# VectorE's tanh rows with the bias in a PSUM bank, and layer 0 through two-bank tiles

## The chip, the cores and the metric

The kernel runs on one core of a Trainium2 chip. Five engines work side by side, each through its own queue in order: TensorE (PE) multiplies matrices into PSUM, VectorE (DVE), ScalarE (ACT) and GpSimd (POOL) work elementwise, and SyncE (SP) starts transfers. Engines wait for one another by semaphores. PSUM is eight banks of 128 partitions by 512 float32 values. The metric is the device time of the whole program in microseconds; lower is better. Everything is float32.

## What is computed

Eight batches of N = 1024 tokens with C = 128 channels pass two layers. Cut to what matters:

```python
# layer 0, per batch, 8 heads; 1024 keys = 64 (m) x 16 (g)
scores = einsum('bhlfc,bhmgc->bhlfmg', q, k) / sqrt(c)
a = softmax(scores, axis=4)        # over m
a = softmax(a, axis=5)             # over g
z = einsum('bhlfmg,bhmgc->bhlfc', a, v)
z1 = layer_norm(z @ wo.T + bo + x)
x = layer_norm(relu(z1 @ w1.T + b1) @ w2.T + b2 + z1)

# layer 1, attention: every pair of tokens i, j
Wi = B @ W.T                       # B: normalised tokens
scores = einsum('d,bijd->bij', v, tanh(Wi[:, None] + Wi[:, :, None]))
t = t + softmax(scores) @ B

# layer 1, recurrence over the 1024 tokens
y = sigmoid(wx_t + y @ V.T)
```

The costly parts are layer 0's double softmax (8 x 8 x 1024 x 1024 scores) and layer 1's tanh of every pair's sum in 128 channels. The pair matrix is symmetric, so only its upper half is computed.

## The kernel before

**Two layers at once.** The kernel doesn't run its loops in order. Functions layer0(b) and layer1(b) only register operations in a Plan (add): which engines may do it and at what cost in us, which keys it reads and writes, its priority, and which tile of a choice (Bank) it takes or gives back. When all are registered, Plan.emit plays a list scheduler at build time: at each step it takes the engine that can start first and, among its ready operations, the one of lowest priority number, and issues it there. So each engine's order is fixed when the program is built, from the costs written in the code, and layer 0 of batch b + 1 is woven among layer 1 of batch b. An operation that gives several engines goes to the one that can start it first. Operations marked port on VectorE and all of GpSimd are planned never to overlap (port_free).

**Layer 0.** For each head the query projection u (L833, evicted with its bias at L837 or L839) and the values (L847, copied at L793 or L795) are made. Then for each tile of 128 queries: scores into a PSUM tile sc of two banks (L869, two matmuls of 512 columns); exponential in place in PSUM (L872, ACT); sums over m and their reciprocal (L876, L877, VectorE), division from PSUM into the SBUF tile e (L880, VectorE). For each pair of such tiles: exponential (L890), sums over g and reciprocal (L893, L894), division on GpSimd (L904), transposes in groups of four through one PSUM bank (L783) and copies out (L795), the product with the values (L918) and its addition to zs (L925). There are two score tiles sc0 and sc1, used in turn, two single banks m0 and m1 for every other product (the choice called two), and two pairs of e tiles. Batch 0's first half runs before any layer 1, and may also use the two banks of sa and the ACT engine for its copies. through_bank is the helper that does a matmul into a bank and its eviction; most products go through it. Batches 0 and 7 do the upper half of their queries first.

**Layer 1's tanh rows.** For each tile it of 128 tokens (w = 1024 - 128 it columns remain), group(...) handles k tokens of each of four interleaved columns c, where k = max(1, 1024 // w): 1, 1, 1, 1, 2, 2, 4, 8 for the eight tiles. Its 4k rows of sums Wi[j] + Wi[i] are written into one of five row slots th, 4096 columns wide. The first of four operations, one for each c, settles whether ACT makes the whole group (tanh_row, L1029: a tanh with the row's own column as bias, one instruction a row) or whether GpSimd and VectorE make the sums, c by c: add_rows (L1039, one instruction for k rows) on GpSimd, and on VectorE where k is 4 or more, which is then marked port; add_row (L1033, one accumulating instruction a row) on VectorE where k is below 4. Sums made there go through one wide tanh (wide_tanh, L1087, ACT). Then times_v (L1107, PE) multiplies by the vector v into the PSUM tile sa of two banks, four column groups side by side, and gives the slot back. After a tile pair's rows comes the exponential from sa to E (L1203), transposes and the product with B (L1236). The result, and layer 1's projections, use the same single banks.

**After the batches** the recurrence runs over all tokens in 32 chunks side by side (L1419, L1421).

PSUM is full: sa 2 banks, sc0 and sc1 2 each, m0 and m1 1 each.

Of the kernel before, what the change touches and what calls it, by code (L numbers as in the profile page):

```python
# [565 lines left out]
def fast_path(ctx: ExitStack, tc: tile.TileContext, a: dict, fits):  # L566
# [67 lines left out]
    m1 = tile_of(psum, "m1", [P, 512])  # L634
    two = (("m0", m0), ("m1", m1))
    four = two + (("sa0", sa[:, 0:512]), ("sa1", sa[:, 512:1024]))
# [82 lines left out]
    for h in range(H):  # L719
        nc.tensor.matmul(m1[:, 0:1], wo[:, h, :], bvn[:, h : h + 1], start=h == 0, stop=h == H - 1)  # L720
    nc.vector.scalar_tensor_tensor(zb, m1[:, 0:1], float(M), bo, ALU.mult, ALU.add)
# [51 lines left out]
    def through_bank(pe, weight, r, evict, where, more, w, pri, choice=two):  # L773

        bank = Bank(*choice)
        n = len(plan.ops)
        add(("PE", weight), lambda _: pe(bank()), r=r, w=[("bank", n)], pri=pri, take=bank, wait=more + w)
        add(where, lambda e: evict(e, bank()), r=[("bank", n)] + more, w=w, pri=pri, give=bank)
# [8 lines left out]
    def copy(dst):  # L787
        def fn(e, bank):
            src = bank
            if len(dst.shape) == 3:  # L790
                src = bank[:, : dst.shape[1] * P].rearrange("p (t c) -> p t c", c=P)
            if e == "ACT":
                nc.scalar.activation(dst, src, AF.Copy)  # L793
            else:
                nc.vector.tensor_copy(dst, src)  # L795
# [6 lines left out]
    def layer0(b):  # L802
# [16 lines left out]
        for n_part, part in enumerate(parts):  # L819
            qts = range(NT) if part is None else range(4 * part, 4 * part + 4)  # L820

            banks = four if alone and n_part == 0 else two
            for h in range(H):
# [5 lines left out]
                for s in range(2) if part is None else (part,):  # L829
                    cols = slice(s * 512, (s + 1) * 512)  # L830

                    def project(bank, h=h, cols=cols):
                        nc.tensor.matmul(bank, A[:, h, :], xT[:, cols], start=True, stop=True)  # L833

                    def biased(e, bank, h=h, u=u, cols=cols):
                        if e == "ACT":
                            nc.scalar.activation(u[:, cols], bank, AF.Identity, bias=ub[:, h : h + 1])  # L837
                        else:
                            nc.vector.tensor_scalar(u[:, cols], bank, ub[:, h : h + 1], None, ALU.add)  # L839

                    through_bank(project, 0.9, [kx], biased, evict(0.75), [], [("u", h % 2, s)], L0, banks)
                for s in () if alone and n_part else range(2):

                    def values(bank, h=h, s=s):
                        for i in range(4):
                            t = 4 * s + i
                            nc.tensor.matmul(  # L847
                                bank[:, i * P : (i + 1) * P], xT[:, t * P : (t + 1) * P], Wvo[:, h, :], start=True, stop=True
                            )

                    through_bank(
                        values, 0.95, [kx], copy(vp[:, 4 * s : 4 * s + 4, :]), evict(0.68), [], [kvp + (s,)], L0, banks
                    )
                for qt in qts:
                    L0 = pace(n_part, h + (qt - qts[0]) / len(qts))
                    i = (n_part * H + h) * len(qts) + qt - qts[0]
                    sc, kc = scs[i % 2], ("sc", i % 2)
# [4 lines left out]
                    r1, r2 = st[:, q, 0:G], st[:, :, G : G + M]  # L862
                    sc3 = sc.rearrange("p (m g) -> p m g", g=G)
                    e3 = e.rearrange("p (m g) -> p m g", g=G)

                    def scores(_, sc=sc, u=u, qt=qt):
                        for s in range(2):
                            cols = slice(s * 512, (s + 1) * 512)
                            nc.tensor.matmul(sc[:, cols], u[:, qt * P : (qt + 1) * P], xT[:, cols], start=True, stop=True)  # L869

                    add(("PE", 1.74), scores, r=[kx, ("u", h % 2, qt // 4)], w=[kc], pri=L0)
                    add(("ACT", 0.98), lambda _, sc=sc: nc.scalar.activation(sc, sc, AF.Exp, scale=SCALE),  # L872
                        r=[kc], w=[kc], pri=L0)

                    def first_sums(_, sc=sc, r1=r1):
                        nc.vector.tensor_reduce(r1, sc.rearrange("p (m g) -> p g m", g=G), AX.X, ALU.add)  # L876
                        nc.vector.reciprocal(r1, r1)  # L877

                    def divide(_, e3=e3, sc3=sc3, r1=r1):
                        nc.vector.tensor_tensor(e3, sc3, r1.unsqueeze(1).to_broadcast([P, M, G]), ALU.mult)  # L880

                    add(("DVE", 1.49), first_sums, r=[kc], w=[k1], pri=L0)
                    add(("DVE", 1.22), divide, r=[kc, k1], w=[ke], pri=L0)
# [15 lines left out]
                    for q in range(2):  # L899
# [7 lines left out]
                        for s in range(2):  # L907
                            through_bank(
                                transposes([e[:, t * P : (t + 1) * P] for t in range(4 * s, 4 * s + 4)]), 0.52, [ke],
                                copy(aT[:, 4 * s : 4 * s + 4, q * P : (q + 1) * P]), evict(0.68), [],  # L910
                                [("aT", na, q, s)], L0, banks,
                            )
# [14 lines left out]
                    for s in range(2):  # L927
                        add(
                            ("PE", 1.74), lambda _, attend=attend, s=s: attend(s),
                            r=[kvp + (p,) for p in range(2)] + [("aT", na, q, p) for q in range(2) for p in range(2)],  # L930
# [5 lines left out]
            for qh in range(2) if part is None else (part,):  # L936
# [24 lines left out]
                kh = [("aT", na, q, s) for q in range(2) for s in range(2)]  # L961
                for f in range(NFF):

                    def hidden(bank, f=f, z1T=z1T):
                        nc.tensor.matmul(bank, w1_sb[:, f * P : (f + 1) * P], z1T, start=True, stop=True)

                    def relu(e, bank, f=f, hT=hT):
                        if e == "ACT":
                            nc.scalar.activation(hT[:, f, :], bank, AF.Relu, bias=b1_sb[:, f : f + 1])
                        else:  # L970
                            nc.vector.tensor_scalar(hT[:, f, :], bank, b1_sb[:, f : f + 1], 0.0, ALU.add, ALU.max)

                    through_bank(hidden, 0.9, [k1], relu, evict(0.75), kh[:1] if f else [], kh if f == 0 else [kh[f]], L0, banks)
# [20 lines left out]
                add(("PE", 5.4), outer, r=kh + [k1], w=[kb], pri=L0, take=bank, wait=[kg])  # L994
# [8 lines left out]
    unused = stats[5][:, 3, 8:9]  # L1003
    slots = [(f"th{s}", ths[s]) for s in range(5)]

    def group(it, at0, r0, k, wiT, all_wi, L1, ROWS, fillers, chain, left, both, first_half):
# [9 lines left out]
        slot = Bank(*slots[: 3 if first_half else 5])  # L1016

        begin = [0 if r0 == 0 else 4 * r0 + c for c in range(4)]
        at = [k * sum(w - q for q in begin[:c]) for c in range(5)]

        def rows(c):
            return slot()[:, at[c] : at[c + 1]].rearrange("p (r n) -> p r n", r=k)

        def w_i(c, r=None):
            j = i0 + 4 * r0 + c
            return wiT[:, j : j + 4 * k - 3 : 4] if r is None else wiT[:, j + 4 * r : j + 4 * r + 1]

        def tanh_row(c, r):
            nc.scalar.activation(rows(c)[:, r, :], wiT[:, i0 + begin[c] :], AF.Tanh, bias=w_i(c, r))  # L1029

        def add_row(c, r):

            nc.vector.tensor_scalar(  # L1033
                rows(c)[:, r, :], wiT[:, i0 + begin[c] :], w_i(c, r), 0.0, ALU.add, ALU.add, accum_out=unused
            )

        def add_rows(eng, c):
# [472 lines left out]
```

## Time and profile before

| | us |
|---|---|
| median of 3 runs | 5395.53 (5393.81 to 5401.85) |
| profiled execution | 5395.36 |
| its span | 5393.6 |
| ACT wide tanh, L1087, x953 | 2629.0 |
| ACT tanh row by row, L1029, x2084 | 1502.5 |
| POOL row adds, L1039, x2268 | 3318.7 |
| DVE row adds one by one, L1033, x1754 | 1542.3 |
| DVE first sums, L876, and division, L880, x512 each | 619.7 and 624.2 |
| DVE copies of 512 columns to aT, L795, x927 | 600.3 |
| PE row products, L1107 | 2037.4 |

The chip's profiler records every instruction with its engine, start and duration. A group's row gives line, engine, operation, what it writes and reads (out<-in), how often, then busy time and mean duration, then the idle time of the engine just before such instructions and what ended most of it. An arrow <- names what was waited for. A float32 matmul appears as two PE instructions in most groups. Busy times are of one execution, and idle time of an engine that isn't the limit costs nothing.

### The profile page before, as it was taken

What the parts mean: (1) busy time and instruction counts of PE and PEld (TensorE: products, weight loads), DVE (VectorE), ACT (ScalarE), POOL (GpSimd) and SP (SyncE); (2) the same over time, 40 slices, a digit from 0 to 9 for tenths busy, and PEclk for the clock granted to TensorE, in tenths of its full rate; (3) what the DMA queues carried; (4) which work ended last, traced back from release to release, by engine and by line L of the source; (5) the groups of instructions that cost most, each with busy time, mean ns of one, the idle gap of its engine ahead of it and who ended that gap; (6) DMA issues with size and microseconds to landing.
All of it is one profiled execution on the core that took longest, in us unless ns stands there. A gap on an engine that the chain in (4) does not pass through costs nothing.

```text
span 5393.6 us, 99434 instructions
## 1 busy us (share of the span) xinstructions
PE 5044.0 (94%) x39173; PEld 2771.6 (51%) x39173; DVE 4933.6 (91%) x8326; ACT 5099.2 (95%) x4190; POOL 4496.0 (83%) x3078
## 2 busy tenths in 40 slices
PE   8999999999999999999999999999999999995566
PEld 6655554555555455555555555545555455542125
DVE  7998989899999999899998999999998999999886
ACT  5489999999999999999999999999999999999994
POOL 2364779798989899899998989898898998996992
PEclk9999999999999999999999999999999999998999
DMA  2000000000000000000000000000000000000001
GB/s 62 1 5 1 1 1 5 1 9 1 1 5 6 4 1 1 5 9 1 1 5 5 5 1 1 5 5 5 1 1 3 7 1 1 1 30 8 1 1 68
DMA packets 27341, 37.73 MB, mean 7 GB/s; under 512 B 2512, under 2 KB 19280, under 8 KB 26864
## 3 DMA queue, kind: packets, MB, share of 16 engines
q1 hardware_dynamic: 24832, 27.99, 1.6%
q8 instruction: 310, 5.08, 0.4%
q10 hardware_dynamic: 1872, 3.16, 0.2%
q14 instruction: 167, 1.37, 0.1%
q0 software_dynamic: 160, 0.13, 0.0%
HBM read 19.22 MB, written 12.06 MB: 6 GB/s over the span
## 4 chain that ended last, share of the span: by engine, by line
PE 56%; ACT 19%; DVE 18%; issue 6%; POOL 1%; DMA 0%; DVEq 0%; ACTq 0%; SPq 0%; POOLq 0%
PE sa L1107 20%; PE m L918 11%; PE sc L869 10%; ACT th L1087 10%; PE m L783 6%; ACT th L1029 5%; DVE th L1033 5%; DVE stat_e L876 2%; DVE stat_e L893 2%; DVE wx L880 2%; ACT sc L872 2%; ACT wx L890 2%; PE m L1236 2%; DVE aT L795 2%; PE m L847 1%
## 5 line engine op out<-in xcount | busy, mean ns | idle before, releaser
L1039 POOL TENSOR_TENSOR th<-wiT 128x1024 f32<-128x1024 f32 (+54 forms) x2268 | 3318.7, 1500 | 318.2 <-PE sa L1107 298.8
L1087 ACT ACTIVATE th<-th 128x4096 f32<-128x4096 f32 (+55 forms) x953 | 2629.0, 2788 | 22.6 <-DVE th L1039 9.5
L1107 PE MATMUL sa<-th,vpat 128*32 128x512 f32 (+33 forms) x24576 | 2037.4, 462 | 235.6 <-ACT th L1087 223.3
L1033 DVE TENSOR_SCALAR_CACHE_REDUCE th<-wiT 128x512 f32<-128x512 f32 (+57 forms) x1754 | 1542.3, 879 | 156.7 <-PE sa L1107 40.3
L1029 ACT ACTIVATE th<-wiT 128x384 f32<-128x384 f32 (+60 forms) x2084 | 1502.5, 792 | 29.2 <-PE sa L1107 28.9
L1107 PEld LDWEIGHTS sa<-th,vpat 128*32 128x32 f32 x24576 | 662.8, 110 | 1372.1 <-issue 844.3
L904 POOL TENSOR_TENSOR wx<-wx,stat_e 128x1024 f32<-128x1024 f32 x512 | 983.9, 1944 | 389.4 <-DVE stat_e L894 320.8
L869 PE MATMUL sc<-xT,wx 128*128 128x512 f32 x2048 | 981.2, 604 | 11.3 <-DVE wx L880 10.7
L918 PE MATMUL m<-aT,wx 128*128 128x256 f32 x3584 | 823.7, 383 | 4.7 <-DVE aT L795 4.5
L918 PEld LDWEIGHTS m<-aT,wx 128*128 128x128 f32 x3584 | 668.1, 190 | 187.5 <-issue 48.0
L880 DVE TENSOR_TENSOR wx<-sc,stat_e 128x1024 f32<-128x1024 f32 x512 | 624.2, 1219 | 25.0
L876 DVE TENSOR_REDUCE stat_e<-sc 128x16 f32<-128x1024 f32 x512 | 619.7, 1210 | 25.8 <-ACT sc L872 25.3
L795 DVE COPY aT<-m 128x512 f32<-128x512 f32 x927 | 600.3, 674 | 36.7 <-PE m L783 34.3
L783 PEld LDWEIGHTS m<-ident,wx 128*128 128x128 f32 x3940 | 443.5, 141 | 326.0 <-issue 156.9
L893 DVE TENSOR_REDUCE stat_e<-wx 128x128 f32<-128x2048 f32 x256 | 583.2, 2278 | 19.1 <-ACT wx L890 18.4
L783 PE MATMUL m<-ident,wx 128*128 128x128 f32 x3940 | 562.6, 278 | 29.7 <-DVE aT L795 14.3
L872 ACT ACTIVATE sc<-sc 128x1024 f32<-128x1024 f32 x512 | 512.7, 1007 | 62.3 <-PE sc L869 56.0
L869 PEld LDWEIGHTS sc<-xT,wx 128*128 128x128 f32 x2048 | 354.7, 190 | 374.4 <-issue 329.3
L890 ACT ACTIVATE wx<-wx 128x2048 f32<-128x2048 f32 x256 | 487.7, 1905 | 30.1 <-DVE wx L880 29.9
L894 DVE RECIPROCAL stat_e<-stat_e 128x128 f32<-128x128 f32 x256 | 243.9, 953 | 8.8
L847 PEld LDWEIGHTS m<-Wvo,xT 128*128 128x128 f32 x1080 | 134.4, 192 | 53.0 <-issue 26.9
L847 PE MATMUL m<-Wvo,xT 128*128 128x128 f32 x1080 | 145.5, 281 | 4.4 <-DVE aT L795 2.4
(183 smaller groups left out, 2887.0 us busy)
## 6 DMA issues: line engine op xcount, KB each, us to landing
xT<-in_xt_dram SPq DMA_DIRECT2D x8, 512.0 KB, 3.6
th<-in_x_dram SPq DMA_DIRECT2D x8, 512.0 KB, 6.8
parked<-X SPq DMA_DIRECT2D x16, 256.0 KB, 2.3
xr<-parked SPq DMA_DIRECT2D x8, 512.0 KB, 8.1
parked_wx<-bT SPq DMA_DIRECT2D x14, 256.0 KB, 2.0
wx<-parked_wx SPq DMA_DIRECT2D x7, 512.0 KB, 4.3
out_dram<-ot ACTq DMA_DIRECT2D x8, 256.0 KB, 2.1
out_dram<-ot SPq DMA_DIRECT2D x8, 256.0 KB, 2.8
```

The lines of the kernel that those rows point to most:

```text
L783: nc.tensor.transpose(bank[:, i * P : (i + 1) * P], s, ident)
L795: nc.vector.tensor_copy(dst, src)
L869: nc.tensor.matmul(sc[:, cols], u[:, qt * P : (qt + 1) * P], xT[:, cols], start=True, stop=True)
L876: nc.vector.tensor_reduce(r1, sc.rearrange("p (m g) -> p g m", g=G), AX.X, ALU.add)
L880: nc.vector.tensor_tensor(e3, sc3, r1.unsqueeze(1).to_broadcast([P, M, G]), ALU.mult)
L904: nc.gpsimd.tensor_tensor(e3, e3, r2[:, q, :].unsqueeze(2).to_broadcast([P, M, G]), ALU.mult)
L918: nc.tensor.matmul(bank()[:, :256], vp[:, t, :], aT[:, t, :], start=t == 0, stop=t == NT - 1)
L1029: nc.scalar.activation(rows(c)[:, r, :], wiT[:, i0 + begin[c] :], AF.Tanh, bias=w_i(c, r))
L1033: nc.vector.tensor_scalar(rows(c)[:, r, :], wiT[:, i0 + begin[c] :], w_i(c, r), 0.0, ALU.add, ALU.add, accum_out=unused)
L1039: eng.tensor_tensor(rows(c), wiT[:, i0 + begin[c] :].unsqueeze(1).to_broadcast(shape), w_i(c).unsqueeze(2).to_broadcast(shape), ALU.add,)
L1087: nc.scalar.activation(slot()[:, a:z], slot()[:, a:z], AF.Tanh)
L1107: nc.tensor.matmul(sa[32 * c : 32 * c + 32, s:s1], vpat[:, 31 - r0 - r : 63 - r0 - r], rows(c)[:, r, s - at0 - begin[c] : s1 - at0 - begin ...
```

## The change

**The bank near.** m1 goes. In its place stands near, one PSUM bank. Its first 64 columns hold layer 0's reciprocals of the first sums; seven areas of 64 columns hold copies of a row tile's own columns of Wi, written by VectorE for each half tile of 64 tokens, in turn. In the profile's operations only VectorE touches it, but for one small product before the plan starts.

**Rows.** VectorE's add is now a tensor_tensor of a broadcast column from near (PSUM) and the other tokens (SBUF), with several rows in one instruction: per = 1, 1, 1, 2, 2, 4, 8, 16 rows for tiles 0 to 7, whoever makes them. A group is cut into 4k / per pieces instead of four, its rows lie token after token, all as long as the longest, and one tanh covers the whole slot. VectorE's row operations are no longer marked port. The matmuls take the same rows at their new places.

**Layer 0.** The first exponential goes from the score tile to e in SBUF, and the score tile is free after it. First sums read e, the reciprocal goes to near, and the division works on e in place. Scores come from the choice called two, which is now sc0 and sc1; so do the eight transposes of a query tile together, the values of a head together, the projection where both halves are made at once, and pairs of hidden products. Each is evicted by one instruction (relu by two) over 1024 columns. Everything narrow takes any of m0, sc0 and sc1. Batch 0's first half may also use sa as a third wide tile.

```diff
+    near = tile_of(psum, "near", [P, 512])
+    two = tuple((f"sc{i}", t) for i, t in enumerate(scs))
+    three = two + (("sa", sa),)
+    any_of = (("m0", m0),) + two
...
-                    sc, kc = scs[i % 2], ("sc", i % 2)
-                    r1, r2 = st[:, q, 0:G], st[:, :, G : G + M]
+                    s1, r2 = st[:, q, 0:G], st[:, :, G : G + M]
+                    r1 = near[:, (2 * pair + q) * G : (2 * pair + q + 1) * G]
...
-                    add(("PE", 1.74), scores, r=[kx, ("u", h % 2, qt // 4)], w=[kc], pri=L0)
-                    add(("ACT", 0.98), lambda _, sc=sc: nc.scalar.activation(sc, sc, AF.Exp, scale=SCALE),
-                        r=[kc], w=[kc], pri=L0)
-                        nc.vector.tensor_reduce(r1, sc.rearrange("p (m g) -> p g m", g=G), AX.X, ALU.add)
-                        nc.vector.reciprocal(r1, r1)
-                        nc.vector.tensor_tensor(e3, sc3, r1.unsqueeze(1).to_broadcast([P, M, G]), ALU.mult)
+                    through_bank(
+                        scores, 1.74, [kx, ("u", h % 2, qt // 4)],
+                        lambda _, bank, e=e: nc.scalar.activation(e, bank, AF.Exp, scale=SCALE), ("ACT", 0.98), [], [ke], L0, wide,
+                    )
+                        nc.vector.tensor_reduce(s1, e.rearrange("p (m g) -> p g m", g=G), AX.X, ALU.add)
+                        nc.vector.reciprocal(r1, s1)
+                        nc.vector.tensor_tensor(e3, r1.unsqueeze(1).to_broadcast([P, M, G]), e3, ALU.mult)
...
-                        for s in range(2):
-                            through_bank(
-                                transposes([e[:, t * P : (t + 1) * P] for t in range(4 * s, 4 * s + 4)]), 0.52, [ke],
-                                copy(aT[:, 4 * s : 4 * s + 4, q * P : (q + 1) * P]), evict(0.68), [],
-                                [("aT", na, q, s)], L0, banks,
-                            )
+                        through_bank(
+                            transposes([e[:, t * P : (t + 1) * P] for t in range(NT)]), 1.04, [ke],
+                            copy(aT[:, :, q * P : (q + 1) * P]), evict(1.24), [], [("aT", na, q)], L0, wide,
+                        )
...
-            nc.vector.tensor_scalar(
-                rows(c)[:, r, :], wiT[:, i0 + begin[c] :], w_i(c, r), 0.0, ALU.add, ALU.add, accum_out=unused
-            )
+        if 4 * r0 % 64 == 0:
+            n = count.setdefault("near", 0)
+            count["near"] = n + 1
+            count["near", it] = n % 7
+            cols, own = near[:, 64 * (n % 7 + 1) : 64 * (n % 7 + 2)], wiT[:, i0 + 4 * r0 : i0 + 4 * r0 + 64]
+            add(("DVE", 0.15), lambda _, cols=cols, own=own: nc.vector.tensor_copy(cols, own), r=all_wi,
+                w=[("near", n % 7)], pri=ROWS - 0.03)
+        kn = ("near", count["near", it])
+        biases = near[:, 64 * (kn[1] + 1) : 64 * (kn[1] + 2)]
+        W = w - 4 * r0
+        per = (1, 1, 1, 2, 2, 4, 8, 16)[it]
+        pieces = 4 * k // per
...
+        def add_rows(e, p):
+            shape = [P, per, W]
+            others = wiT[:, i0 + 4 * r0 :].unsqueeze(1).to_broadcast(shape)
+            if e == "DVE":
+                own = biases[:, 4 * r0 % 64 + p * per : 4 * r0 % 64 + (p + 1) * per].unsqueeze(2).to_broadcast(shape)
+                nc.vector.tensor_tensor(rows(p), own, others, ALU.add)
+            else:
+                own = w_i(p * per, per).unsqueeze(2).to_broadcast(shape)
+                nc.gpsimd.tensor_tensor(rows(p), others, own, ALU.add)
...
         work = {
-            "ACT": lambda c: (k * (0.18 + 0.833e-3 * (w - begin[c])), lambda: [tanh_row(c, r) for r in rows_of]),
-            "POOL": lambda c: (0.27 + 1.62e-3 * k * (w - begin[c]), lambda: add_rows(nc.gpsimd, c)),
-            "DVE": lambda c: (k * (0.21 + 1.05e-3 * (w - begin[c])), lambda: [add_row(c, r) for r in rows_of])
-            if k < 4
-            else (0.15 + 1.04e-3 * k * (w - begin[c]), lambda: add_rows(nc.vector, c)),
+            "ACT": (per * (0.18 + 0.833e-3 * W), lambda p: [tanh_row(j) for j in rows_of(p)]),
+            "POOL": (0.27 + 1.62e-3 * per * W, lambda p: add_rows("POOL", p)),
+            "DVE": (0.15 + 1.04e-3 * per * W, lambda p: add_rows("DVE", p)),
         }
```

## The prediction

> **What bounds the kernel now.** I read the page's busy shares first, then the same per stretch (windows), then the groups of the stretch from 310 to 4650 us, then those of the end, and last the durations of single lines.
>
> ```profile
> PE 5044.0 (94%) x39173; PEld 2771.6 (51%) x39173; DVE 4933.6 (91%) x8326; ACT 5099.2 (95%) x4190; POOL 4496.0 (83%) x3078
> ```
>
> Four engines lie between 83 and 95%, so no share alone tells the bound. The windows do (columns: stretch, length, then busy us and instructions of PE, PEld, DVE, ACT, POOL, the granted clock, DMA):
>
> ```profile
> 0.00:100.00 100.00, 91.27 (x449) 69.88 (x450) 67.94 (x87) 62.04 (x180) 26.94 (x25) 1.00 0.30 83
> ...
> 200.00:310.00 110.00, 101.04 (x449) 67.20 (x447) 98.50 (x138) 57.85 (x66) 47.12 (x32) 1.00 0.00 1
> ...
> 2000.00:2500.00 500.00, 490.52 (x3804) 266.80 (x3802) 464.18 (x790) 495.47 (x390) 460.27 (x317) 1.00 0.01 4
> ...
> 4700.00:4900.00 200.00, 169.92 (x1464) 84.26 (x1466) 186.39 (x456) 192.19 (x153) 173.37 (x126) 0.95 0.08 25
> ...
> 5000.00:5100.00 100.00, 59.82 (x536) 16.39 (x536) 84.19 (x152) 100.00 (x34) 90.46 (x57) 0.98 0.00 1
> ```
>
> The reader sees four regimes. Start, 0 to 310: layer 0 of batch 0 alone; PE 91%, DVE 90% once loaded. Middle, 310 to 4700: PE 98% and ACT 99% together, DVE 93%, POOL 92%. End, 4700 to 5300: only layer 1 of batch 7 is left at last; ACT near 100%, PE 60%. From 5300 the recurrence, untouched. Summed over its windows, PE is busy 4278.6 of the middle's 4390 us: 111 us idle. Which waits those are, and who else waits, is in the groups of 310 to 4650:
>
> ```profile
> L1039 POOL TENSOR_TENSOR th<-wiT 128x832 f32<-128x832 f32 (+54 forms) x1915 | 2812.2, 1505 | 248.1 <-PE sa L1107 239.5 <-ACT th L1029 5.2 <-ACT sc L872 1.5
> L1107 PE MATMUL sa<-th,vpat 128*32 128x512 f32 (+36 forms) x20688 | 1692.0, 458 | 56.3 <-ACT th L1087 53.6 <-ACT E L1203 1.6 <-ACT th L1029 0.8
> L869 PE MATMUL sc<-xT,wx 128*128 128x512 f32 x1792 | 859.5, 604 | 9.3 <-DVE wx L880 9.1
> L783 PE MATMUL m<-ident,wx 128*128 128x128 f32 x3588 | 512.7, 278 | 23.4 <-DVE aT L795 12.4 <-DVE wx L839 4.4 <-POOL E L1209 2.6
> ```
>
> POOL waits 240 us for PE to give a row slot (th) back, so the rows are made faster than PE eats them: PE is the bound of the middle, and the rows that ACT makes itself (L1029) fill its time. PE idles half because a tanh came late (56), the rest because a PSUM bank was not yet emptied (L783, L869). The end:
>
> ```profile
> L1087 ACT ACTIVATE th<-th 128x2804 f32<-128x2804 f32 (+47 forms) x200 | 526.3, 2702 | 15.7 <-DVE th L1033 7.5 <-DVE th L1039 7.1 <-POOL th L1039 0.6
> L1029 ACT ACTIVATE th<-wiT 128x448 f32<-128x448 f32 (+41 forms) x141 | 83.7, 667 | 0.0
> ```
>
> There ACT is the bound; it waits 15 us for adds and spends 84 us on 141 rows one by one. The prices of VectorE's forms:
>
> ```profile
> L1033 DVE TENSOR_SCALAR_CACHE_REDUCE th<-wiT 128x512 f32<-128x512 f32 x26 | 19.3, 743 | 1.4 <-DVE th L1033 0.3
> L1033 DVE DVE_READ_ACCUMULATOR th<-wiT 128x1 f32 x1754 | 144.7, 82 | 0.0
> L880 DVE TENSOR_TENSOR wx<-sc,stat_e x512: 1160/1224/1226, 33.0 to 4761.5; 128x1024 f32<-128x1024 f32 x171
> L1039 DVE TENSOR_TENSOR th<-wiT x94: 394/1147/5540, 539.3 to 4944.3; 128x1024 f32<-128x1024 f32 x13, 128x760 f32<-128x760 f32 x5, 128x832 f32<-128x832 f32 x4, 128x564 f32<-128x564 f32 x4
> ```
>
> A row by the accumulating form costs 743 + 82 ns at 512 columns. L880 (one input in PSUM, one in SBUF) never leaves 1160 to 1226 ns; L1039 on VectorE (both inputs in SBUF) goes up to 5540.
>
> [...]L876 (PSUM, 1024) takes 1210 ns and L893 (SBUF, 2048) 2278; less one element in 1.042 ns[...] both keep about 144.[...]
>
> **The change part by part.** Sums are made on the profiled execution, 5395.36 us with 1.8 outside its span of 5393.6; the median, 5395.53, is the same to 0.01%.
>
> 1. Rows on VectorE. An add with one PSUM input is taken as L880's form: 1219 - 1024 x 1.042 = 152 ns fixed, so 685 at 512 columns against 825: 140 ns a row, x1754 = 246 us of VectorE. Row groups of tiles 3 to 7 save more, as 2 to 16 rows share one instruction and VectorE need no longer be kept off the widest ones. Against it 128 copies of 64 bias columns (2 a row tile, 8 tiles, 8 batches); the smallest L795 copy, 128 columns, is 227 ns, and an estimate of 160 gives 20 us. That a broadcast PSUM input runs at one element a cycle is not shown; L880 broadcasts its SBUF input. If it were half as fast the rows would lose 1.04 ns x some 640 columns x 1754 = 1.2 ms; I see no reason for it and take 0.
> 2. Wide tiles in layer 0. 927 + 128 copies of 512 become half as many of 1024: one fixed part of 674 - 533 = 141 ns less per pair, 74 us. The projection's 96 evictions of batches 1 to 6 become 48, some 10 us. Relu still issues two, and PE's matmuls stay one for one: nothing.
> 3. The first exponential to SBUF. ACT: L872 is 1007 ns to PSUM, L1203's 1024 columns from PSUM to SBUF are 1.00 us: nothing. First sums: strided from SBUF. [...]L1405 reads 256 strided elements in 532 ns, less L1033's 210 fixed this is 1.26 ns an element, +0.22 x 1024 = 225 ns. [...]I take 0. Divide: still one PSUM and one SBUF input, 0.
> 4. Rows of a group are all as long as its first: up to 3 columns more for ACT, 1416 a batch, x 0.833 ns (L1087's slope: 4096 columns, 3613 ns) x 8 = 9 us of ACT. PE's four column groups run beside one another[...]: 0.
> 5. Banks. Before: two 2-bank tiles for scores alone, held from the matmul through exp, sum and divide; two single banks for all else. After: sc0, sc1 and m0, of which wide work may take only the first two. Scores give the tile back after exp, so each tile is free 1210 + 253 + 1219 ns, and what those waited, sooner; but 8 transposes, projection and values now hold such a tile through a 1.2 us copy. Per pair of query tiles (627 us a batch / 32 = 19.6 us) I estimate scores 2 x 5, transposes 2 x 4 and projection plus values 2.5 = 20.5 us on two tiles, 52% of 39: before it was about 2 x 9.5, 48%, with the single banks near 70%. About even, and the narrow work has three places.
> 6. The tile e is held from the exponential instead of the divide, some 4 us longer. In the timeline near 2600 one pair lives from 2599.9 to 2624.4, 24.5 us; with 4 more 28.5 against two periods of 39. In the start 25 second exponentials (L890) run between 33 and 310 us, a period of 11.1 us, so the two pairs are tight there; I take no gain there, and -10 to +10.
>
> VectorE sum: -246 - 84 + 20 = -310 of 4934 us. None of this is on PE, so it counts only through what PE and ACT wait for. If the planner gives the freed time to rows that ACT makes now (792 ns, some 711 columns; 890 ns on VectorE), 348 rows move, and ACT saves 0.2 us of fixed part on each: 70 us.
>
> Middle: of PE's 111 idle us I take half, 50: tanh come earlier (ACT less full) and copies start sooner (VectorE at 87 instead of 93%). It can't exceed 111, since PE's work is unchanged; below, 0. End: ACT's waits for adds 15 plus 141 rows x 0.2 = 28, together 43; I take 25, since from 5000 us on ACT does nothing but wide tanh and has nothing to give. Start 0. Sum -75: 5320 us. What is late next: PE itself in the middle, ACT's wide tanh at the end.
>
> **The rivals.** A, more is won: nearly all of the 111 and the 43, and 10 at the start: about 5260. For it: VectorE rows stand 1.1 us apart for 755 columns and 0.70 for 328 in the timeline, so the real saving is larger than 140 ns. Against: PE would have to be at 99.5%. B, nothing: PE's order was laid down with slack already, its gaps are the difference between plan and chip, and stay: 5390. For it: POOL's 240 us of waiting for slots. C, slower: the shared two-bank tiles. About 512 scores, 512 wide transposes and 128 projections and values wait for sc0 or sc1; PE takes its orders in sequence, so when ACT or VectorE empties a tile later than planned everything behind stops, row matmuls too. At 0.1 us each 115 us, less 75: 5435. It decides from 0.065 us a use. For it: PE already waits 35 us for evictions with six places, and now there are four; ACT works in pieces of 3 us and a score tile waits behind one. Against: half the evictions, and the earlier release.
>
> **How the numbers follow.** Forecast (5290 to 5370) 0.46, A 0.18, B 0.10, C 0.26. No change means within 0.2%, 11 us, which is what a measurement tells apart. From B 0.08 is no change and 0.02 a small gain; C counts as slower whole, giving 0.66, 0.08, 0.26. The range cuts A at 5262 and C at 5435, leaving about 0.08 and 0.11 outside; the likeliest case's own range is 5290 to 5370.
>
> **What would show it.** Right: VectorE's accumulating form gone, its row adds at N x 1.042 + 150 ns with no long outliers; fewer single-row tanh on ACT; VectorE's busy time some 300 us less for the same rows; PE idle in the middle near 60 us. Wrong: PE idle before scores and transposes, released by ACT's exponential or the copies, above 110 us in the middle (C); first sums clearly over 1210 ns; adds from PSUM slower than 1.04 ns an element; or a start longer than 320 us.

## The result, and the profile after

The changed kernel takes 5546.95 us (median of 4 runs, 5540.44 to 5548.38) against 5398.69 us before (4 runs, 5393.81 to 5402.65): ratio 1.0277, 95% interval 1.0265 to 1.0289. It is slower by 148 us, where 75 us less was forecast. The span of its profiled execution is 5546.5 us.

Below stand the chain of work that ended last in the kernel before, by engine; then, of the kernel after, the busy time of each engine and that chain, by engine and by line.

```profile
PE 56%; ACT 19%; DVE 18%; issue 6%; POOL 1%; DMA 0%; DVEq 0%; ACTq 0%; SPq 0%; POOLq 0%
```

```profile
PE 5049.0 (91%) x39173; PEld 2807.4 (51%) x39173; DVE 5127.7 (92%) x5657; ACT 5055.3 (91%) x3888; POOL 4447.8 (80%) x2704
...
DVE 55%; PE 25%; ACT 10%; issue 8%; POOL 1%; DMA 0%; DVEq 0%; SPq 0%; ACTq 0%; POOLq 0%
DVE stat_e L885 14%; DVE th L1056 12%; PE sa L1110 8%; DVE stat_e L902 7%; DVE wx L889 7%; ACT th L1090 7%; DVE aT L798 6%; PE sc L877 4%; PE m L925 4%; PE sc L784 2%; PE sc L925 2%; DVE stat_e L903 2%; DVE near L886 2%; ACT th L1049 2%; DVE wx L798 1%
```

The bound has moved. Before, the chain was 56% PE and 18% DVE; now it is 55% DVE, and its largest single item is L885, the first sums. VectorE issues a third fewer instructions (5657 against 8326), and is busy 194 us longer.

The group of the first sums before (L876), and the groups of VectorE after (busy us and mean ns, then idle time just before):

```profile
L876 DVE TENSOR_REDUCE stat_e<-sc 128x16 f32<-128x1024 f32 x512 | 619.7, 1210 | 25.8 <-ACT sc L872 25.3
...
L1056 DVE TENSOR_TENSOR th<-near,wiT 128x912 f32<-128x912 f32 (+50 forms) x1380 | 1509.5, 1133 | 141.6 <-PE sa L1110 136.5
L885 DVE TENSOR_REDUCE stat_e<-wx 128x16 f32<-128x1024 f32 x512 | 990.6, 1935 | 43.6 <-ACT wx L881 43.2
L889 DVE TENSOR_TENSOR wx<-near,wx 128x1024 f32<-128x1024 f32 x512 | 624.2, 1219 | 12.3
```

The division (L889) takes what it took (1219 ns). The rows (L1056) are cheaper: before, L1033 covered 1555.5 us of the span and L1039 on VectorE 126.5, together 1682; now the rows cover 1509.5 and the bias copies 28.8. (Time covered is less than the sum of the durations where records overlap.) But the first sums went from 1210 to 1935 ns, 619.7 to 990.6 us, and that alone is +371.

The timeline of the kernel after in its middle (start, duration, instruction) shows how this meets the order that the plan laid down:

```profile
2610.81 1.95 DVE L885 TENSOR_REDUCE stat_e<-wx 128x16 f32<-128x1024 f32 x1 [1.55 <-ACT wx L881]
2612.79 0.26 DVE L886 RECIPROCAL near<-stat_e 128x16 f32<-128x16 f32 x1
2613.09 1.23 DVE L889 TENSOR_TENSOR wx<-near,wx 128x1024 f32<-128x1024 f32 x1
2614.23 2.01 DVE L1056 TENSOR_TENSOR th<-near,wiT 128x864 f32<-128x864 f32 x2
2616.16 2.03 DVE L885 TENSOR_REDUCE stat_e<-wx 128x16 f32<-128x1024 f32 x1
```

And of before, near the same time:

```profile
2612.38 1.22 DVE L876 TENSOR_REDUCE stat_e<-sc 128x16 f32<-128x1024 f32 x1
2613.62 0.25 DVE L877 RECIPROCAL stat_e<-stat_e 128x16 f32<-128x16 f32 x1
2613.98 1.22 DVE L880 TENSOR_TENSOR wx<-sc,stat_e 128x1024 f32<-128x1024 f32 x1
```

From the start of the sums to the start of the division is 2613.09 - 2610.81 = 2.28 us after, and 2613.98 - 2612.38 = 1.60 before. The plan that fixes every engine's order still charges 1.49 for them, so what is behind them on VectorE comes some 0.7 us later than it did, 512 times.

Who waits for that is in PE's groups from 310 to 4650 us, the stretch that the prediction showed of before:

```profile
L1110 PE MATMUL sa<-th,vpat 128*32 128x512 f32 (+27 forms) x19648 | 1596.3, 461 | 45.9 <-ACT th L1090 42.3 <-ACT E L1206 2.9
L877 PE MATMUL sc<-xT,wx 128*128 128x512 f32 x1756 | 852.4, 612 | 37.3 <-DVE aT L798 23.4 <-ACT wx L881 5.6 <-DVE wx L847 4.5
L925 PE MATMUL m<-aT,wx 128*128 128x256 f32 x2320 | 537.8, 385 | 23.1 <-DVE aT L798 22.6
L784 PE MATMUL sc<-ident,wx 128*128 128x128 f32 x3536 | 468.8, 279 | 84.5 <-DVE aT L798 34.4 <-DVE wx L798 18.0 <-POOL wx L913 9.2
```

PE's waits for a tanh have not grown (56.3 to 45.9). Its waits for transposes (23.4 to 84.5) and scores (9.3 to 37.3) have, and VectorE's copies (L798) release most of them: the copies are not longer (1208 ns for 1024 columns, and 1210 in e1 below, where the sums are fast), they stand behind slower sums.

The windows of after (stretch, length, busy us and instructions of PE, PEld, DVE, ACT, POOL, clock, DMA) say where:

```profile
200.00:310.00 110.00, 87.61 (x366) 59.52 (x364) 92.10 (x112) 47.77 (x49) 42.63 (x29) 0.89 0.00 1
...
2000.00:2500.00 500.00, 477.77 (x3829) 266.22 (x3831) 484.56 (x547) 479.49 (x358) 439.59 (x271) 1.00 0.01 4
...
5100.00:5200.00 100.00, 58.00 (x581) 15.94 (x577) 79.02 (x74) 100.00 (x33) 92.38 (x55) 0.97 0.00 1
```

In the middle DVE is now at 97% (93 before), PE at 96 (98) and ACT at 96 (99). From 200 to 310 us PE does less too, 87.6 of 110 us against 101.0. The end looks as before: ACT at 100%.

### The profile page after: what moved, and what is told of

Same layout as the page of the kernel before. It is cut to its first block, busy times and chain, and to the rows that moved or that the text cites. A ratio compares the mean times of both kernels' runs of the same rounds, so it can differ in the third digit from the quotient of the medians.

```text
span 5546.5 us, 95345 instructions
## 1 busy us (share of the span) xinstructions
PE 5049.0 (91%) x39173; PEld 2807.4 (51%) x39173; DVE 5127.7 (92%) x5657; ACT 5055.3 (91%) x3888; POOL 4447.8 (80%) x2704
## 4 chain that ended last, share of the span: by engine, by line
DVE 55%; PE 25%; ACT 10%; issue 8%; POOL 1%; DMA 0%; DVEq 0%; SPq 0%; ACTq 0%; POOLq 0%
DVE stat_e L885 14%; DVE th L1056 12%; PE sa L1110 8%; DVE stat_e L902 7%; DVE wx L889 7%; ACT th L1090 7%; DVE aT L798 6%; PE sc L877 4%; PE m L925 4%; PE sc L784 2%; PE sc L925 2%; DVE stat_e L903 2%; DVE near L886 2%; ACT th L1049 2%; DVE wx L798 1%
## 5 line engine op out<-in xcount | busy, mean ns | idle before, releaser
L1059 POOL TENSOR_TENSOR th<-wiT 128x1536 f32<-128x1536 f32 (+44 forms) x1894 | 3269.4, 1759 | 376.4 <-PE sa L1110 342.3
L1090 ACT ACTIVATE th<-th 128x3392 f32<-128x3392 f32 (+49 forms) x996 | 2738.6, 2787 | 44.6 <-DVE th L1056 23.8
L1110 PE MATMUL sa<-th,vpat 128*32 128x512 f32 (+25 forms) x24576 | 2006.0, 460 | 225.6 <-ACT th L1090 208.1
L1056 DVE TENSOR_TENSOR th<-near,wiT 128x912 f32<-128x912 f32 (+50 forms) x1380 | 1509.5, 1133 | 141.6 <-PE sa L1110 136.5
L913 POOL TENSOR_TENSOR wx<-wx,stat_e 128x1024 f32<-128x1024 f32 x512 | 981.8, 1939 | 528.3 <-DVE stat_e L903 434.9
L1049 ACT ACTIVATE th<-wiT 128x512 f32<-128x512 f32 (+53 forms) x1796 | 1348.7, 818 | 56.8 <-PE sa L1110 54.8
L885 DVE TENSOR_REDUCE stat_e<-wx 128x16 f32<-128x1024 f32 x512 | 990.6, 1935 | 43.6 <-ACT wx L881 43.2
L889 DVE TENSOR_TENSOR wx<-near,wx 128x1024 f32<-128x1024 f32 x512 | 624.2, 1219 | 12.3
L784 PE MATMUL sc<-ident,wx 128*128 128x128 f32 x3984 | 529.8, 279 | 104.6 <-DVE aT L798 35.5
L798 DVE COPY aT<-sc 128x1024 f32<-128x1024 f32 x478 | 571.7, 1208 | 8.9 <-PE sc L784 7.7
L881 ACT ACTIVATE wx<-sc 128x1024 f32<-128x1024 f32 x503 | 505.8, 1011 | 66.5 <-PE sc L877 57.5
```

What stands on the lines that cost most here:

```text
L784: nc.tensor.transpose(bank[:, i * P : (i + 1) * P], s, ident)
L885: nc.vector.tensor_reduce(s1, e.rearrange("p (m g) -> p g m", g=G), AX.X, ALU.add)
L889: nc.vector.tensor_tensor(e3, r1.unsqueeze(1).to_broadcast([P, M, G]), e3, ALU.mult)
L913: nc.gpsimd.tensor_tensor(e3, e3, r2[:, q, :].unsqueeze(2).to_broadcast([P, M, G]), ALU.mult)
L1049: nc.scalar.activation(rows()[:, j, :], wiT[:, i0 + 4 * r0 :], AF.Tanh, bias=w_i(j))
L1056: nc.vector.tensor_tensor(rows(p), own, others, ALU.add)
```

## The experiments

Three theories. S: the strided read of SBUF in the first sums makes the loss; its halves are S1, the 371 us of added work on VectorE, and S2, a plan laid out with the old price. B: layer 0's new flow (shared two-bank tiles, e held longer) makes it. The third is that the rows' part costs. Each ratio is to runs of the kernel before on the same chip.

One thing limits all readings. A change of prices or of what waits for what makes the planner lay out another order. In the traces every engine of the kernel after, of e1 and of e6 has the same instructions in the same order, so these three differ in how the first sums read e, and in nothing else; e4 has the order of before, but for one instruction of VectorE at the very start. Each of the other runs has an order of its own, and its time includes what that order does. How much that can be is seen below: e10 and e11 lie 53 us apart.

**e1 and e6: as many sums of as many elements, read otherwise.** Neither computes the right sums: e1 adds 64 neighbours, e6 64 words at a stride of two.

```diff
-  nc.vector.tensor_reduce(s1, e.rearrange("p (m g) -> p g m", g=G), AX.X, ALU.add)
+  nc.vector.tensor_reduce(s1, e.rearrange("p (g m) -> p g m", g=G), AX.X, ALU.add)   # e1
+  nc.vector.tensor_reduce(s1.rearrange("p (a g) -> p a g", g=2),
+      e.rearrange("p (a m g) -> p a g m", a=G // 2, g=2), AX.X, ALU.add)             # e6
```

> The changed kernel with the first sums reading e contiguously, 64 neighbouring elements per sum, so each sum is over the wrong elements; count, engines and plan are the same. Theory S (the strided SBUF read costs VectorE 0.73 us in each of 512 first sums): the sums fall from 1.94 to about 1.21 us and the time to 5300 to 5400 us, where the prediction had put the change. Theory B (the shared two-bank tiles stop PE): the time stays at 5500 us or more.

> The changed kernel with the first sums reading every second element (16 sums of 64 elements with a stride of two words in place of sixteen), each sum over the wrong elements. [...]the sums take 1.21 us and the time is 5330 to 5365 us; if every hop that leaves the neighbouring word is slow, 1.9 us or more and 5540 us or more.

e1: 5346.01 us (5344.93 to 5347.45), ratio to before 0.991 (0.9894 to 0.9927). e6: 5346.92, 0.9907 (0.989 to 0.9923). The first range of e6's expectation is for a stride of two words that keeps the rate; the runs have strides of 4, 8 and 64 bytes, and none lies between 8 and 64. Below, of e1, the busy line of its profile, its chain and the group of the sums; then the sums' line of e6 (min/median/max ns).

```profile
PE 4999.4 (94%) x39173; PEld 2791.7 (52%) x39173; DVE 4783.4 (89%) x5657; ACT 5029.8 (94%) x3888; POOL 4441.1 (83%) x2704
...
PE 58%; ACT 22%; DVE 10%; issue 8%; POOL 2%; DMA 0%; ACTq 0%; SPq 0%; DVEq 0%; POOLq 0%
...
L885 DVE TENSOR_REDUCE stat_e<-wx 128x16 f32<-128x1024 f32 x512 | 616.8, 1205 | 75.1 <-ACT wx L881 70.4
```

```profile
L885 DVE TENSOR_REDUCE stat_e<-wx x512: 1159/1219/1656, 31.4 to 4738.8; 128x16 f32<-128x1024 f32 x171
```

One access pattern decides the sign: 201 us, and the chain is PE's again. The instruction is the same in number, size, place and waits, so it is the read itself. (The clock granted to PE, 0.986 in the profiled execution of after and 0.992 in e1's, differs by 0.6%, the times by 3.8%.) Every second word is nearly as good as every word (means of 1231 and 1205 ns); every sixteenth isn't (1935 in the kernel after). PE's waits in the same stretch of e1 go back to what they were before:

```profile
L877 PE MATMUL sc<-xT,wx 128*128 128x512 f32 x1816 | 870.9, 606 | 9.8 <-ACT wx L881 4.4 <-DVE aT L798 4.2 <-DVE E L1216 0.6
...
L784 PE MATMUL sc<-ident,wx 128*128 128x128 f32 x3645 | 476.6, 277 | 18.4 <-POOL wx L913 6.9 <-DVE aT L798 4.7 <-DVE wx L798 3.0
```

**e4: the slow read alone, in the kernel before.** The sums read xT in SBUF with the same stride, in place of the score tile, and the reciprocal reads 16 exponentials of the score tile, so the softmax's right divisors are left out; all else stays.

```diff
-  nc.vector.tensor_reduce(r1, sc.rearrange("p (m g) -> p g m", g=G), AX.X, ALU.add)
-  nc.vector.reciprocal(r1, r1)
+  nc.vector.tensor_reduce(r1, xT.rearrange("p (m g) -> p g m", g=G), AX.X, ALU.add)
+  nc.vector.reciprocal(r1, sc[:, 0:G])
```

> The kernel before with one cost added alone: the first sums read the batch's transposed tokens in SBUF with the same stride of 16 elements, and the reciprocal reads 16 exponentials of the score tile, so the softmax's divisors are wrong; the plan is the same. Theory S: each sum goes from 1.21 to 1.94 us, VectorE gets 370 us more in all, and the time rises to 5500 to 5650 us. Theory B: the sums' length matters little, below 5440 us.

5666.52 us (5665.19 to 5667.3), 1.0505 (1.0487 to 1.0522). Its group in the list by line:

```profile
L876 DVE TENSOR_REDUCE stat_e<-xT 128x16 f32<-128x1024 f32 x512 | 990.7, 1935 | 1.8 <-DMA xT<-in_xt_dram 1.8
```

The same 1935 ns, from a tile that nothing writes at that time, and some 272 us, more than either theory had. So the price belongs to the strided read of SBUF, not to e, its exponential or a wait. A read of PSUM with the same stride doesn't pay it: 1210 ns in before (L876) and 1208 in e2 (L887), against 1205 for the contiguous read of SBUF in e1.

**e5 and e9: the plan is told the price.** In both, one number; e5 is the kernel after, e9 is e4.

```diff
-  add(("DVE", 1.49), first_sums, r=[ke], w=[k1], pri=L0)
+  add(("DVE", 2.21), first_sums, r=[ke], w=[k1], pri=L0)
```

> The changed kernel with the planner's cost of the first sums raised from 1.49 to 2.21 us, what the chip takes; the instructions are the same. Theory S1 (the 371 us of extra work on VectorE are the cost): the time stays within 40 us of 5547. Theory S2 (the harm is that the order was laid out with a wrong price): below 5470 us, half of the loss against the run with contiguous sums comes back.

> The kernel before with the slow strided sums (wrong divisors, as in the run that added this cost alone, 5666 us) and the planner's cost of them raised from 1.49 to 2.21 us. Theory S2 (more than half of the loss comes from an order laid out with the wrong price): 5470 to 5560 us. Theory S1 (the work itself): 5630 us or more.

e5: 5424.39 us, 1.005 (1.0033 to 1.0067). e9: 5446.44 us, 1.0086 (1.0068 to 1.0104). Of e5, the chain by engine and the group of the sums:

```profile
PE 49%; ACT 27%; DVE 14%; issue 8%; POOL 2%; DMA 0%; ACTq 0%; POOLq 0%; DVEq 0%; SPq 0%
...
L885 DVE TENSOR_REDUCE stat_e<-wx 128x16 f32<-128x1024 f32 x512 | 991.8, 1937 | 73.0 <-ACT wx L881 69.5
```

VectorE does the same slow sums, yet 123 of the 201 us come back: told the price, the planner gives VectorE 1197 row pieces instead of 1380 and ACT 2040 single rows instead of 1796, and VectorE's share of the chain falls from 55 to 14%. What is left to e1, 78 us, is what the work costs once it is planned for. From the other side, in the kernel before, it is 220 and about 47 us. S2 is more than half in both, and e9 came out even below the range that it was given. Both runs also got a new order; no run with another false price tells how much of the gain any new order would have brought.

**e3 and e7: the rows as before**, in the kernel after and in e1.

```diff
-            "DVE": (0.15 + 1.04e-3 * per * W, lambda p: add_rows("DVE", p)),
+            "DVE": lambda c: (k * (0.21 + 1.05e-3 * (w - begin[c])), lambda: [add_row(c, r) for r in rows_of])
+            if k < 4
+            else (0.15 + 1.04e-3 * k * (w - begin[c]), lambda: add_rows(nc.vector, c)),
...
-        for p in range(pieces):
+        for c in range(4):
```

> The changed kernel with the tanh rows made as before (accumulating adds on VectorE, one instruction a row, four pieces by column); layer 0 is as changed. Theory S: the rows are the change's good half, so without them it is slower than the changed kernel, 5580 to 5700 us. If instead the row adds from PSUM or their longer pieces were the fault, it is below 5500 us.

> Layer 0 as changed with contiguous (wrong) first sums, and the tanh rows as before: the wide tiles and the exponential to SBUF alone, without the strided read. Theory B (shared two-bank tiles cost PE time by themselves): 5420 us or more, above the kernel before. Otherwise 5370 to 5400 us, and the 5346 us with both parts is then the rows' gain.

e3: 5698.68 us (5694.51 to 5701.89), 1.0562 (1.0544 to 1.058). e7: 5425.29 us (5420.62 to 5426.36), 1.0049 (1.0032 to 1.0066). The rows' part gains: 152 us where VectorE is the bound (e3 to after), 79 us where PE is (e7 to e1). And e7 is the rest of the change with the stride's price taken out: not a gain, as forecast, but a loss of 0.3 to 0.7%, 17 to 36 us. By its own expectation this is B's side, in a small part; but a new order alone can move as much. The stretch from 500 to 4700 us in before and then in e7 (columns as above) has PE 36 us less busy:

```profile
500.00:4700.00 4200.00, 4094.14 (x32028) 2236.32 (x32027) 3915.08 (x6417) 4142.37 (x3193) 3760.62 (x2566) 1.00 0.01 3
...
500.00:4700.00 4200.00, 4057.81 (x31689) 2250.51 (x31688) 3875.13 (x5874) 4096.56 (x3162) 3602.38 (x2456) 0.99 0.01 3
```

**e2, e10, e11: which part of layer 0's flow?** e2 keeps the first exponential in the shared tile, so that sums and division read PSUM and the tile is held through the division. e10 is e1 with the transposes in fours through any of three tiles, copied 512 columns at a time. e11 is e10 with the scores' matmul not waiting for e; their exponential, which writes e, waits instead.

```diff
-  lambda _, bank, e=e: nc.scalar.activation(e, bank, AF.Exp, scale=SCALE), ("ACT", 0.98), [], [ke], L0, wide,
+  add(("PE", 1.74), lambda _, scores=scores, bank=bank: scores(bank()), r=[kx, ("u", h % 2, qt // 4)],
+      w=[kb], pri=L0, take=bank, wait=[ke])
+  add(("ACT", 0.98), first_exp, r=[kb], w=[kb], pri=L0)
+  add(("DVE", 1.49), first_sums, r=[kb], w=[k1], pri=L0)
+  add(("DVE", 1.22), divide, r=[kb, k1], w=[ke], pri=L0, give=bank)                 # e2
...
-  transposes([e[:, t * P : (t + 1) * P] for t in range(NT)]), 1.04, [ke],
+  transposes([e[:, t * P : (t + 1) * P] for t in range(4 * s, 4 * s + 4)]), 0.52, [ke],   # e10
...
-  through_bank(scores, 1.74, ...)
+  scores_to(scores, 1.74, ...)                                                      # e11
+  def scores_to(pe, weight, r, evict, where, more, w, pri, choice):
+      bank = Bank(*choice)
+      n = len(plan.ops)
+      add(("PE", weight), lambda _: pe(bank()), r=r, w=[("bank", n)], pri=pri, take=bank)
+      add(where, lambda e: evict(e, bank()), r=[("bank", n)], w=w, pri=pri, give=bank)
```

> The changed kernel with layer 0's first exponential again in place in PSUM, first sums and division from PSUM, the score tile held through the division; rows, wide copies and shared tiles stay. Theory S: first sums at 1.21 us and 5330 to 5420 us. Theory B: the shared tiles are held longer still, so at least 5550 us.

> The changed kernel with contiguous (wrong) first sums and with the transposes again four at a time, through any of m0, sc0 and sc1, copied 512 columns at a time. If the copies through the two shared two-bank tiles are what the changed layer 0 loses on PE (theory B), it is faster than 5346 us; if halving the copies is what pays, VectorE gets some 70 us more and the time is 5360 to 5400 us.

> e10 (first sums contiguous, transposes in fours, 512-wide copies), with one more change: the score matmul no longer waits for the buffer e to be free (it writes PSUM only); the exponential, which is what writes e, waits for it instead. Computes what e10 computes, first sums wrong as in e1. If the matmul's wait for e is what layer 0's part costs against the kernel before (e7 was 28 us above it), TensorE no longer stands there: below 5340 us, down to 5325. If the planner's order keeps e free by then anyway and the wait never ends last: 5346 to 5356, as e10.

e2: 5485.50 us, 1.0171 (1.0154 to 1.0188). e10: 5350.57 us (5350.19 to 5351.83), 0.9909 (0.9892 to 0.9926). e11: 5403.97 us (5399.99 to 5407.78), 1.0012 (1.0005 to 1.0019). e2 pays no stride (its sums read PSUM) and still loses 139 us to e1; it lies between the ranges of S and B. What its edit adds is the holding: its transposes, in the list by line of e2, now wait for divisions (L892), which give the tile back:

```profile
L784 PE MATMUL sc<-ident,wx 128*128 128x128 f32 x4032 | 544.5, 281 | 58.5 <-DVE wx L892 30.8 <-DVE aT L798 10.5 <-POOL wx L919 9.9
```

In e1 the same group waits 28.5 us in all. The difference is a part of the 139 us; that the holding makes the rest, through the new order, is argued. So the early release of the score tile is probably what makes shared tiles affordable. The width of the transposes decides little: e10 is 4.6 us above e1, and in neither of its expected ranges. e11 missed both of its expectations: taking PE's wait away cost 53 us. Between the two, single-row tanhs rose from 1848 to 1952, and PE was busy for 4066.75 us of the stretch 500 to 4700 against 4106.09. A tile that is taken before its e is free is a tile held longer, like e2's; that this is the reason is argued, not shown, since the plan's whole order changed with it. What makes up layer 0's 17 to 36 us stays open: neither narrow transposes nor taking PE's wait for e away won anything back.

**e8 and e12: a version that keeps the gain.** e8 lays a query's keys out in pairs (key order a, m, g with 16 = 8 x 2), so that the first sums read every second word, as in e6, and the right ones. The host's transposition of x is laid out so; the projection reads its tokens in natural order through an access pattern, the second sums take one reduction a query tile, and both divisions broadcast over pairs. e12 is e8 with e10's and e11's edits.

```diff
-  nc.vector.tensor_reduce(s1, e.rearrange("p (m g) -> p g m", g=G), AX.X, ALU.add)
+  nc.vector.tensor_reduce(s1.rearrange("p (a g) -> p a g", g=2), e.rearrange("p (a m g) -> p a g m", a=G // 2, g=2), AX.X, ALU.add)
...
-  nc.gpsimd.tensor_tensor(e3, e3, r2[:, q, :].unsqueeze(2).to_broadcast([P, M, G]), ALU.mult)
+  by_key = r2[:, q, :].unsqueeze(1).unsqueeze(3).to_broadcast([P, G // 2, M, 2])
+  nc.gpsimd.tensor_tensor(pairs(e), pairs(e), by_key, ALU.mult)
...
-  "xt": np.asarray(x).reshape(NB, N, C).transpose(0, 2, 1),
+  "xt": np.asarray(x).reshape(NB, N // 16, 8, 2, C).transpose(0, 4, 2, 1, 3).reshape(NB, C, N),
```

> The changed kernel with the keys kept in another order, so that the right first sums read every second word: key m*16 + 2a + g lies at a*128 + 2m + g in the transposed tokens, the scores and e; the second sums read pairs of neighbouring words and are one instruction for each query tile. By the stride-2 run the first sums take 1.23 us; if the second sums and GpSimd's division keep their rate (1.2 us for 1024, 1.94 us), the time is 5340 to 5370 us, faster than both kernels. If one of them loses its rate in the new order, 5400 us or more.

> e8 (keys laid out in pairs, the reference computed) with the narrow transposes of e10 and the score matmul not waiting for e. If the wait costs what layer 0's part lost: below 5345 us (e8 was 5357). If it does not: 5352 to 5366, the narrow transposes being even with the wide ones and the division on GpSimd still at about 2150 ns.

e8: 5357.37 us (5353.84 to 5359.79), 0.992 (0.9902 to 0.9938): 0.8% faster than the kernel before, clear of noise, and 3.4% faster than the kernel after. e12: 5416.15 us, 1.0038 (1.0024 to 1.0052), which missed both of its expectations and repeats e11's loss on another base. Of e8, from the list by line:

```profile
L891 DVE TENSOR_REDUCE stat_e<-wx 128x16 f32<-128x1024 f32 x512 | 629.4, 1229 | 66.1 <-ACT wx L887 64.4 <-POOL th L1072 0.2
...
L921 POOL TENSOR_TENSOR wx<-wx,stat_e 128x1024 f32<-128x1024 f32 x512 | 1088.9, 2149 | 345.6 <-DVE stat_e L911 317.2 <-ACT th L1318 7.0 <-DVE stat L743 7.0
```

The sums are back at full rate. The layout is paid on GpSimd (2149 instead of 1939 ns, 107 us in all) and in second sums (598.0 us busy instead of 583.0), and of that 11 us reach the end. GpSimd's division did lose its rate, for which 5400 us or more were expected; that the time fell in the other range is luck, and GpSimd, 85% busy, had the room.

## Why the prediction was wrong

The direction failed at one term. By its own steps:

1. *Rows on VectorE, -246 us.* About right. The add from PSUM, with its PSUM operand broadcast, takes 1214 ns for 1024 columns, where L880's form, the price taken, took 1219. In the list by form, and then by line, after (the second line: min/median/max ns of all forms):

```profile
L1056 DVE TENSOR_TENSOR th<-near,wiT 128x1024 f32<-128x1024 f32 x26 | 30.9, 1214 | 2.3 <-PE sa L1110 2.2
...
L1056 DVE TENSOR_TENSOR th<-near,wiT x1380: 679/1085/2292, 312.5 to 5444.1; 128x864 f32<-128x864 f32 x9, 128x912 f32<-128x912 f32 x6, 128x816 f32<-128x816 f32 x5, 128x1008 f32<-128x1008 f32 x4
```

   No outlier of 5.5 us is left: pieces of 2048 elements, the largest, take 2280 ns in the mean, and the longest record is 2292, where L1039 on VectorE went up to 5540; what made those long no run isolates. Row work with the bias copies covers 1682 - 1538 = 144 us less than before, and VectorE makes more rows in it: by the output sizes of the records, 1.306 million elements a partition against 1.199 million. Per element that is 1.18 ns instead of 1.40, or some 270 us for the rows of before, where 226 were forecast. Two errors in the sum work against each other. The 82 ns that I added for reading the accumulator lie almost wholly inside the add's own record (L1033's two kinds sum to 1687 us in the list and cover 1555), and the pieces of several rows save more than the sum has. The copies are 225 ns each, not 160.
2. *Wide copies, -84.* Too large: L795 and L839 covered 759.5 + 81.1 us, in e1 L798 and L847 cover 715.3 + 75.3, so 50 (some 63 for the same number of columns, since VectorE copies 1.6% more of them in e1).
3. *First sums from SBUF, "I take 0".* **This is the step that failed.** It is +371 us, over three times the most that the prediction's own estimate allows, 225 ns x 512 = 115 us. That estimate came from L1405: 532 ns, less 210 fixed, over 256 elements. The 210 belonged to another instruction, the accumulating add. With the fixed 144 ns of L876 and L893 (1024 elements more are 2278 - 1210 = 1068 ns more, 1.04 an element), the sums' 1935 ns give (1935 - 144) / 1024 = 1.75 ns an element; at that rate 256 elements take 448, and L1405 keeps 84 ns of fixed part: that line held the right price, and the borrowed fixed part hid it (worked out, not tested). The move to SBUF alone gives next to nothing: read contiguously from there the sums take 1205 ns (e1), only 5 less than from PSUM. Nor was 0 a neutral choice, when the only strided SBUF read on view pointed up. At three strides in SBUF the sums took 1205 ns (one word, e1), 1231 and 1229 (two, e6 and e8) and 1935 (sixteen, the kernel after); why, no run shows.
   The step also left out a second cost: that the plan's 1.49 would then be wrong. By e5 and e9 this was more than half of what the stride cost. Of the signs of being wrong that the prediction lists, first sums clearly over 1210 ns is the one that named the cause.
4. *Row length, +9 us of ACT.* The count is right: the records of after have 11328 more row elements than those of before, 8 x 1416. What they cost ACT no run isolates, nor what they cost PE; PE's row products do overlap (before, 24576 records of 462 ns in the mean cover 2037.4 us).
5. *Banks, about even*, and rival C. Even, as taken: with full-rate sums PE waits 18.4 + 9.8 us for transposes and scores, before 23.4 + 9.3. The sign for C (PE idle before these) did appear in the kernel after, and C's mechanism with it: tiles were emptied late, by VectorE's copies. But what made them late was the slow sums, which C didn't have; with full-rate sums these waits are as before. C's direction came true through a cost that it didn't name.
6. *e held longer, no gain at the start, -10 to +10.* Not isolated. In the first 310 us PE is busy 12 us less in both e1 and e7 than before, but the first tanh rows begin earlier there (at 282 and 277 us, before at 306), while batch 0's last product with the values begins later in e1 (451 us, before 411). That PE itself waits for e to be free was missed; e11 shows that its removal doesn't help.

The sums of the prediction: VectorE -310 was +194 in the kernel after, and -150 in e1, where it also makes 9% more row elements and ACT 288 fewer single rows (348 were forecast). With the stride gone, e1 stands at 5346 where 5320 was forecast, inside the likeliest case's own range of 5290 to 5370. That number is right in part by luck. Half of PE's idle time in the middle was to go, 50 us; it went from 111 to 108. The spans of before and e1 differ by 48 us and PE's busy times by 45, and PE's work was what the prediction held fixed. And "PE is the bound of the middle" was true before; it was taken to stay true, with VectorE at 93% and only savings written against it. 371 us on an engine with some 7% free is a new bound.

## What to carry to other kernels

When data moves from PSUM to SBUF, price each later read by its access pattern as well as its size: float32 sums of 1024 elements that read SBUF at a stride of 64 bytes took 1935 ns here, and 1205 read contiguously; from PSUM the same stride took 1210. Don't bound an unknown form with another form's fixed part; and where an order is planned from prices, a wrong price costs a second time, so correct it before judging the change itself.

## What was not expected

- A wrong number in the plan cost more (123 of 201 us; 220 of 272) than the slow work it hid.
- VectorE's records overlap: where nothing is waited for, an instruction's record can end some 0.08 us after the next has begun. In the timeline of after, the division starts at 2613.09 and lasts 1.23, yet the next starts at 2614.23. Sums of durations overstate what a saved instruction gives.
- PE's own busy time isn't fixed: 5044.0 us before, 4999.4 in e1, for the same 39173 instructions. By line, the transposes cover 671.7 us before and 627.6 in e1, the row products 2037.4 and 2007.6 (lines overlap, so these don't add up). The transposes go with their width: eight at a time they cover 627 to 648 us in all runs, four at a time 661 to 697. The row products go only loosely with the layout of the rows: 2022 to 2040 us with rows as before, 2006 to 2030 as after. Why they differ stays open; part may be the granted clock, which from 4700 us on is 0.94 before and 0.97 in e1.
